# Batch 0 of the experts' layer computed for its chosen tokens only, its routing inside the first attention

## The chip, the cores and the metric

The kernel runs on one core of a Trainium2 chip. Its five engines (TensorE for matrix products, VectorE or DVE, ScalarE or ACT, GpSimd or POOL, and SyncE, which issues most DMAs) run their own instruction queues in order and meet at semaphores. The metric is the device time of one execution in microseconds (us), as the median of several.

## The reference

Two layers over `x` of shape (4, 512, 128). Each normalizes `x`, computes an attention `s` and a feed-forward gate `g` from it, and adds `s * silu(g)`. The change concerns the feed-forward part of the second layer, a mixture of 8 experts of which each token uses its best two:

```
xt = x.reshape(-1, d)                       # d = 128, 512 tokens for each of 4 batches
g = gelu(xt @ wg1 + bg1)
probs = softmax(g @ wg2)                    # 8 experts
top_vals, top_idx = top_k(probs, 2)
gates = zeros_like(probs).at[n, top_idx].set(top_vals)
h = gelu(einsum('nd,edh->enh', xt, w_in))   # hidden width 256
o = einsum('enh,ehd->end', h, w_out)
y = einsum('ne,end->nd', gates, o)
```

The first layer's attention works through segments of 64 tokens with a running memory (16 heads of 64); its own experts come before it. The second layer's attention has 16 heads of 8 and sums a softmax over 16 channels.

## The kernel before

The stages follow each other: the first layer's experts, the first attention, the second layer's experts, the second attention. A batch has 512 tokens in four tiles of 128. Nearly every instruction is issued through a helper (`mm1`, `act1`, `vec1`, `pool1`, `dma1`, lines 335 to 347) that keeps it in program order on its engine, so the order written in the code is the order of each queue.

**The first attention**, `attn0` (line 568), runs 32 segments, eight for each batch, in one loop. Segment n computes the scores of n+1, reads and updates the memory, attends, and turns the result of segment n-2. Segments with n % 4 other than 2 also hold four chunks of the projections of a later pair of tiles (values, keys, then queries); from segment 27 on there are none left. Segments with n % 4 = 2, from 6 on, end with an `output`, which adds two finished tiles to `x`. Work of the next stage is hung in with a table `between`: a key n means at the end of segment n, n - 0.5 ahead of its `attend`, n - 0.25 behind its chunks. PSUM is shared out by tags: "t" has two buffers of 512 values, "w" has three of 1024.

**The second layer's experts**, `begin_ffn1` (line 877), route a batch in steps: `sums`, `roots` and `scale` (statistics; `roots` is a square root on ACT), `normed`, `turned` (transposed on TensorE), `split` (three bf16 parts, on POOL), `hidden` (with GELU), `logits` (with an exponential), `chosen` (the best two, on DVE). From there two ways lead on.

- Batch 0 is dense: `up` and `down` (lines 1000 and 1010) compute all tokens for each of the eight experts, and DVE adds each expert's result with its weight (lines 1023 and 1025).
- Batches 1 to 3 compute chosen tokens: `placed` (line 1029) counts each token's place with its expert, `marked` (1051) makes 0/1 matrices from the places, `send` (1060) gathers the tokens of a tile with three bf16 products into 64 places per expert, `up2` and `down2` (1075 and 1086) compute two experts at once and write rows to DRAM, `fetch` (1103) reads each token's two rows back with indirect DMAs on POOL, and `joined` (1118) weighs and adds them on DVE. If an expert had more tokens in a tile than places, a flag starts another path at the end.

`ffn1` (line 1131) runs these as steps. A step issues its `up`, then what `between` holds for it, then the `down` of the step before, then what `between` holds half a step later. Before the change there are 20 steps: six dense ones, four of batch 1, two dense ones, four of batch 2, four of batch 3. The first `up` already stands in segment 31 of the attention. In between lie the routes of batches 2 and 3, the marks and sends of batches 1 to 3, the last `output` of the first attention, and fourteen calls of `prepare`, which make the second attention's operands of batch 0 and begin those of batch 1 (`prepare1`, line 1340: token products evicted on DVE, projections evicted on ACT, products of pairs on POOL, products of three (`cubes`) on DVE, and `forms` and `turned` on TensorE). All these use the PSUM tag "t" in turn with `down`, `logits` and `hidden`.

**The second attention**, `attn1`, runs 64 steps of one tile by four heads. Its table `rest` holds the fetches of batches 2 and 3 from steps 20 and 28 and their joins from 33 and 50. `gate1` applies the silu of a batch in the thirteenth step of that batch.

Of the kernel before, what the change touches and what calls it, by code (L numbers as in the profile page):

```python
# [21 lines left out]
P = 128  # L22
# [86 lines left out]
class Kernel:  # L109
# [767 lines left out]
    def begin_ffn1(self, pool, psum, layer, rooms=False):  # L877
# [31 lines left out]
        def chooses(b):  # L909
            return rooms and b > 0  # L910
# [140 lines left out]
        def marked(b, k):  # L1051

            t = marks[b, k] = self.f1b.tile(
                [P, NE, ROOM], BF16, name=name("one", b, k), tag="one", bufs=5
            )
            self.vec1(v.tensor_tensor(
                t, bc(places, 1, NE), bc(place[b][:, k], 2, ROOM), ALU.is_equal
            ))

        def send(b, k):  # L1060

            if k == 0:
                sent[b] = self.second1[b % 2].rearrange("p k (e s) -> p (k e) s", e=2).rearrange(
                    "p e (k s) -> p e k s", k=4
                )
                rows[b] = self.rooms.tile([NE * 4 * ROOM, D], F32, name=name("rows", b))
            ps = psum.tile([P, NE, ROOM], F32, name=name("px", b, k), tag="w", bufs=3)
# [5 lines left out]
            self.act1(sent[b][:, :, k], ps, AF.Copy)  # L1073

        def up2(b, i):
            ps = psum.tile([P, 2, 2, 4 * ROOM], F32, name=name("ph", b, i), tag="w", bufs=3)
            for e in range(2):
                for c in range(2):
                    self.mm1(
                        ps[:, e, c], lhsT=self.w_in[:, 2 * i + e, c * P : (c + 1) * P],  # L1080
                        rhs=sent[b][:, 2 * i + e], start=True, stop=True,
# [21 lines left out]
        def fetch(b, at, n=1):  # L1103

            if at == 0:
                acc[b] = self.of_batch("g", layer, b)
                got[b] = acc[b], (
                    self.first1[0][:, 0].rearrange("p (k d) -> p k d", k=4) if b == 1
                    else self.of_batch("xnT", layer + 4, b - 2)
                )  # L1110
# [20 lines left out]
    def ffn1(self, first, between, begun=False):  # L1131
# [4 lines left out]
        if begun:  # L1136
            dense = [(0, e) for e in range(NE)]
            own = [[(b, e) for e in range(NE // 2)] for b in range(B)]
            steps = dense[:6] + own[1] + dense[6:] + own[2] + own[3]
        for at, (b, e) in enumerate(steps):  # L1140
            up, down = (first.up2, first.down2) if begun and b else (first.up, first.down)
# [748 lines left out]
    def attn1(self, xnT, g1, rest):  # L1890
# [4 lines left out]
        with tc.tile_pool(name="a1", bufs=2) as self.a1, tc.tile_pool(  # L1895
# [70 lines left out]
            for i in range(n):  # L1966
# [3 lines left out]
                if t == 12:  # L1970
                    self.gate1(pool, g1[b], b)
# [333 lines left out]
    def run(self):  # L2305
# [15 lines left out]
        with tc.tile_pool(name="wf1", bufs=1) as wf1, tc.tile_pool(name="f1", bufs=1) as f1:  # L2321
# [7 lines left out]
            with tc.tile_pool(name="ap", bufs=1, space=PSUM) as psum:  # L2329
# [7 lines left out]
                    18: [(first.sums, 0)], 19: [(first.sums, 1)],  # L2337
                    20: [(first.roots, 0, 2)], 20.5: [(first.scale, 0, 2, False), (first.normed, 0)],
                    21: [(first.turned, 0), (first.normed, 1)],
# [134 lines left out]
```

## Time and profile before

| what | us |
|---|---|
| median of 3 runs | 721.2 (721.18 to 721.28) |
| the profiled execution | 722.03 |
| its span from first to last instruction | 720.4 |
| TensorE busy, of the span | 678.1 |
| one matmul of `down` or `down2` (320 in all) | 0.278 |
| one matmul of `up` / of `up2` | 0.595 / 0.379 |
| one indirect fetch on POOL | 0.95 to 1.39 |

A matmul's record overlaps with its neighbours', so the length of a group is read from the start of one group to the start of the next. In the groups of instructions a row gives the line, the engine, the operation, the tile written and the tile read, their shapes and the count; the time in brackets is what the engine waited before it, and for whom. Line 336 and line 339 are helpers, so instructions there are told apart by their tiles: `ph` is the product of `up`, `eo` that of `down`, `px` that of `send`, `lp` the logits, `pn` the places, `sc`, `mm`, `mu` and `dot` belong to a segment of the first attention, and `po` to its `output`. The experts' stage lies between 323 and 433 us of the span, the first attention between 84 and 326, the second from 433 on.

### The profile page before, as it was taken

How to read it: one execution, taken by the hardware profiler on the slowest of the kernel's cores; microseconds unless marked ns; L12 is line 12 of the kernel's file. 1: busy time of each engine (PE TensorE's matmuls, PEld its weight loads, DVE VectorE, ACT ScalarE, POOL GpSimd, SP SyncE). 2: the span in 40 equal slices, each digit the busy share in tenths (PEclk: the TensorE clock that was granted, in tenths of full speed). 3: DMA queues.
4: the chain of work that ended last, by engine and by line, in shares of the span. 5: the costliest groups of instructions: out<-in, count | busy, mean ns of one | idle time of the engine just before them, and what ended most of it. 6: DMA issues, size and time to landing. Idle time of an engine off the chain costs nothing.

```text
span 720.4 us, 23270 instructions
## 1 busy us (share of the span) xinstructions
PE 678.1 (94%) x9888; PEld 418.1 (58%) x9891; DVE 503.7 (70%) x1078; ACT 490.9 (68%) x809; POOL 345.7 (48%) x381
## 2 busy tenths in 40 slices
PE   7999879999999899979999999999999999999994
PEld 4666557878879677867777783332335233422433
DVE  6776365667576775884549324889896999588854
ACT  3423457877777885653563468989987899899830
POOL 7680027566666574693754423411482844312250
PEclk9999999999999998999999999999999999999999
DMA  7740143231331312100034249967949494955200
GB/s 184 135 134 0 56 129 79 67 106 40 97 106 33 105 30 78 39 12 1 1 98 153 74 146 213 255 168 174 240 148 221 109 250 129 217 143 144 59 17 19
DMA packets 84847, 79.42 MB, mean 110 GB/s; under 512 B 42512, under 2 KB 73520, under 8 KB 81664
## 3 DMA queue, kind: packets, MB, share of 16 engines
q1 hardware_dynamic: 81904, 75.12, 39.6%
q0 software_dynamic: 2256, 2.47, 1.8%
q8 instruction: 80, 1.31, 0.8%
q10 hardware_dynamic: 576, 0.26, 0.1%
q14 instruction: 31, 0.25, 0.1%
HBM read 51.62 MB, written 26.21 MB: 108 GB/s over the span
## 4 chain that ended last, share of the span: by engine, by line
PE 70%; DVE 12%; ACT 10%; issue 4%; DMA 2%; POOL 1%; SPq 0%; DVEq 0%; ACTq 0%; POOLq 0%
PE acc L336 9%; PE pp L336 8%; ACT e L339 7%; PE eo L336 7%; PE po L336 5%; PE ph L336 4%; PE b L336 3%; PE pv L336 3%; PE s L336 3%; PE pl L336 3%; PE sc L336 2%; PE pa L785 2%; PE pg L336 2%; PE pu L336 2%; PE dot L336 2%
## 5 line engine op out<-in xcount | busy, mean ns | idle before, releaser
L339 ACT ACTIVATE e<-s 128x1024 f32<-128x1024 f32 x124 | 121.9, 1056 | 13.8 <-PE s L336 12.7
L336 PE MATMUL acc<-e,strip 128*32 128x512 f32 x1000 | 124.6, 598 | 0.9 <-DVE e L1874 0.9
L339 ACT ACTIVATE e<-e 128x1024 f32<-128x1024 f32 x104 | 107.4, 1094 | 0.0
L736 POOL TENSOR_TENSOR t<-t,gate 128x512 f32<-128x512 f32 x32 | 49.7, 1554 | 66.0 <-DVE t L717 66.0
L336 PEld LDWEIGHTS acc<-e,strip 128*32 128x32 f32 x1000 | 28.6, 109 | 70.4 <-issue 59.2
L774 POOL TENSOR_TENSOR t<-t,gate 128x512 f32<-128x512 f32 x32 | 50.7, 1585 | 31.0 <-DVE sums L773 24.6
L339 ACT ACTIVATE pj<-pp 128x512 f32<-128x512 f32 x64 | 38.5, 602 | 21.2 <-PE pp L336 21.0
L684 DVE SCALAR_TENSOR_TENSOR elu<-elu,up 128x512 f32<-128x512 f32 x60 | 48.0, 801 | 5.3 <-ACT up L339 5.3
L661 DVE TENSOR_TENSOR E<-sc,cap 128x512 f32<-128x512 f32 x32 | 22.0, 688 | 40.2 <-PE sc L336 40.2
L339 ACT ACTIVATE h<-ph 128x1024 f32<-128x1024 f32 x20 | 20.5, 1023 | 38.3 <-PE ph L336 31.0
L339 ACT ACTIVATE attT<-pa 128x128 f32<-128x128 f32 x128 | 25.0, 284 | 28.5 <-PE pa L785 28.1
L336 PE MATMUL s<-q,k 64*128 64x512 bf16 x256 | 40.9, 382 | 3.5 <-ACT e L339 3.3
L336 PEld LDWEIGHTS <-k 64*128 64x128 bf16 x256 | 8.8, 94 | 59.6 <-issue 58.6
L775 POOL TENSOR_TENSOR t<-t,t 128x512 f32<-128x512 f32 x32 | 41.8, 1307 | 2.5
L336 PE MATMUL eo<-w_out,h 128*128 128x128 f32 x320 | 39.6, 278 | 0.0
L336 PEld LDWEIGHTS eo<-w_out,h 128*128 128x128 f32 x320 | 37.6, 192 | 3.4 <-issue 1.9
L339 ACT ACTIVATE elu<-pj 128x512 f32<-128x512 f32 x60 | 38.5, 642 | 0.1
L1714 POOL TENSOR_TENSOR pr<-pr,pr 128x512 f32<-128x512 f32 x14 | 22.5, 1629 | 33.4 <-DVE pr L1709 33.3
L339 ACT ACTIVATE up<-pj 128x512 f32<-128x512 f32 x60 | 38.4, 639 | 0.0
L336 PE MATMUL pp<-xnT,l0Wq 128*64 128x128 f32 x512 | 31.2, 277 | 3.2 <-ACT attT L339 2.2
L1623 DVE TENSOR_TENSOR second<-second,first 128x1024 f32<-128x1024 f32 x16 | 27.0, 1694 | 9.0 <-DMA second<-qf 9.0
L1157 POOL TENSOR_SCALAR th<-th 128x512 f32<-128x512 f32 x4 | 2.5, 617 | 64.2 <-ACT th L339 64.2
(331 smaller groups left out, 1641.9 us busy)
## 6 DMA issues: line engine op xcount, KB each, us to landing
vd<-vt SPq DMA_DIRECT2D x32, 256.0 KB
vone<-vd SPq DMA_DIRECT2D x64, 128.0 KB
first<-qe SPq DMA_DIRECT2D x8, 1024.0 KB
second<-qf SPq DMA_DIRECT2D x16, 512.0 KB
third<-qf SPq DMA_DIRECT2D x32, 256.0 KB
qf<-qT SPq DMA_DIRECT2D x64, 64.0 KB
k<-kd SPq DMA_DIRECT2D x16, 256.0 KB
q<-qd SPq DMA_DIRECT2D x16, 256.0 KB
```

The lines of the kernel that those rows point to most:

```text
L336: return self.pin(self.nc.tensor.matmul(*args, **kw))
L339: return self.pin(self.nc.scalar.activation(*args, **kw))
L661: self.vec1(nc.vector.tensor_tensor(e, ps[:, :, 0:256].rearrange("p x (hp c) -> p x hp c", hp=4), bc(bc(self.cap, 1, 4), 1, 2), ALU.min,))
L684: self.vec1(nc.vector.scalar_tensor_tensor(t, t, 1.0, up, ALU.min, ALU.add))
L736: nc.gpsimd.tensor_mul(t, t, self.gate)
L774: nc.gpsimd.tensor_mul(t, t, gate2)
L775: nc.gpsimd.tensor_add(t, t, seg[n]["t1"])
L785: self.pin(nc.tensor.transpose(ps[:, hp, :], seg[n]["att"][:, hp].rearrange("i p v -> i (p v)"), self.ident,))
L1157: self.pool1(self.nc.gpsimd.tensor_scalar(t, t, 0.5, 0.5, ALU.mult, ALU.add))
L1623: self.vec1(self.nc.vector.tensor_mul(t, t, self.first1[mm][:, two]))
L1714: self.nc.gpsimd.tensor_add(self.prod1[b, m], self.prod1[b, m], t)
```

## The change

Batch 0 takes the second way as well. The code of the diff, cut to its core:

```diff
         def chooses(b):
-            return rooms and b > 0
+            return rooms
...
         def marked(b, k):
-            t = marks[b, k] = self.f1b.tile(
-                [P, NE, ROOM], BF16, name=name("one", b, k), tag="one", bufs=5
-            )
+            if b == 0:
+                if k % 2 == 0:
+                    marks[b, -1] = self.top.tile(
+                        [P, 2, NE, ROOM], BF16, name=name("one", b, k), tag=f"g{k // 2}"
+                    )
+                t = marks[b, k] = marks[b, -1][:, k % 2]
+            else:
+                t = marks[b, k] = self.f1b.tile(
+                    [P, NE, ROOM], BF16, name=name("one", b, k), tag="one", bufs=5
+                )
...
         def send(b, k):
             if k == 0:
-                sent[b] = self.second1[b % 2].rearrange("p k (e s) -> p (k e) s", e=2).rearrange(
-                    "p e (k s) -> p e k s", k=4
-                )
+                if b:
+                    sent[b] = [self.second1[b % 2].rearrange("p k s -> p (k s)")]
+                else:
+                    sent[b] = self.wqkv[0:2]
+                each = NE // len(sent[b])
+                sent[b] = [t.rearrange("p (e k s) -> p e k s", e=each, k=4) for t in sent[b]]
...
-            ps = psum.tile([P, NE, ROOM], F32, name=name("px", b, k), tag="w", bufs=3)
+            tag, bufs = ("w", 3) if b else ("t", 2)
+            ps = psum.tile([P, NE, ROOM], F32, name=name("px", b, k), tag=tag, bufs=bufs)
...
-            self.act1(sent[b][:, :, k], ps, AF.Copy)
+            each = NE // len(sent[b])
+            for n, t in enumerate(sent[b]):
+                self.act1(t[:, :, k], ps[:, n * each : (n + 1) * each], AF.Copy)
...
             if at == 0:
                 acc[b] = self.of_batch("g", layer, b)
-                got[b] = acc[b], (
-                    self.first1[0][:, 0].rearrange("p (k d) -> p k d", k=4) if b == 1
-                    else self.of_batch("xnT", layer + 4, b - 2)
-                )
+                got[b] = [acc[b]]
+            if at == 4:
+                got[b].append(self.of_batch("xnT", layer + 4 + b // 2, b % 2))
...
-            dense = [(0, e) for e in range(NE)]
-            own = [[(b, e) for e in range(NE // 2)] for b in range(B)]
-            steps = dense[:6] + own[1] + dense[6:] + own[2] + own[3]
+            steps = [(b, i) for b in range(B) for i in range(NE // 2)]
...
-                if t == 12:
-                    self.gate1(pool, g1[b], b)
+                if t == 4 and b or i == n - 4:
+                    self.gate1(pool, g1[b - (t == 4)], b - (t == 4))
...
-                    18: [(first.sums, 0)], 19: [(first.sums, 1)],
-                    20: [(first.roots, 0, 2)], 20.5: [(first.scale, 0, 2, False), (first.normed, 0)],
-                    21: [(first.turned, 0), (first.normed, 1)],
-                    21.5: [(first.turned, 1), (first.split, 1)],
-                    21.75: [(first.hidden, 0), (first.hidden, 1)],
-                    23: [(first.logits, 0), (first.logits, 1), (first.chosen, 1)],
-                    24: [(first.placed, 1)], 25: [(first.chosen, 0)],
-                    30.5: [(first.up, 0, 0)],
+                    11: [(first.sums, 0)], 13.75: [(first.roots, 0, 1)],
+                    14: [(first.scale, 0, 1, False), (first.normed, 0)],
+                    15: [(first.turned, 0)], 16: [(first.split, 0)], 17.75: [(first.hidden, 0)],
+                    18.5: [(first.logits, 0)], 19: [(first.sums, 1)], 19.5: [(first.chosen, 0)],
+                    20: [(first.roots, 1, 2)], 20.5: [(first.scale, 1, 2, False), (first.normed, 1)],
+                    21: [(first.turned, 1), (first.placed, 0)],
+                    21.5: [(first.split, 1)], 21.75: [(first.hidden, 1)],
+                    22: [(first.marked, 0, 0)], 22.5: [(first.marked, 0, 1)],
+                    23: [(first.logits, 1)], 23.5: [(first.chosen, 1)],
+                    24.5: [(first.marked, 0, 2)], 25: [(first.placed, 1)], 25.5: [(first.marked, 0, 3)],
+                    26: [(first.send, 0, 0)], 27: [(first.send, 0, 1), (first.sums, 2)],
+                    28: [(first.send, 0, 2)], 28.75: [(first.roots, 2, 3)], 29: [(first.send, 0, 3)],
+                    30.5: [(first.up2, 0, 0)],
...
+                    1: [(f.scale, 2, 3, False), (f.normed, 2)],
+                    2: [(left[0],), (f.turned, 2), (f.split, 2)],
+                    3: [(f.hidden, 2), (left[1],), (begin,)] + marks(1, 0, 1, 2, 3),
+                    3.5: sends(1, 0, 1, 2, 3),
+                    4: [(f.logits, 2), (f.sums, 3), (f.chosen, 2)],
+                    5: [(f.roots, 3, 4)], 5.5: [(f.placed, 2)],
+                    6: marks(2, 0, 1) + [(f.scale, 3, 4, False), (f.normed, 3)],
+                    7: [(f.turned, 3)] + marks(2, 2, 3) + sends(2, 0, 1), 7.5: sends(2, 2, 3) + [(f.split, 3)],
+                    8: [(f.hidden, 3)], 9: [(f.logits, 3), (f.chosen, 3)],
+                    10.5: [(f.placed, 3)] + marks(3, 0, 1), 11: marks(3, 2, 3) + sends(3, 0, 1),
+                    11.5: sends(3, 2, 3), 13: [(self.operands1, 0, m) for m in range(3)],
+                    14: [(f.up2, B - 1, NE // 2 - 1), (self.opening1, psum, "w", 3)],
+                    15.5: [(self.opened1, psum, "w", 3)],
...
-                for k in range(14):
-                    between.setdefault(5 + k, []).append((prepare,))
+                for at in (4, 4, 5, 6, 6, 7, 8, 9, 9, 10, 10, 11, 12, 13):
+                    between.setdefault(at, []).append((prepare,))
                 for k in range(4):
-                    between.setdefault(13 + k, []).append((f.fetch, 1, 2 * k, 2))
+                    between.setdefault(7 + k, []).append((f.fetch, 0, 2 * k, 2))
...
-        for b, at, then in ((2, 20, 33), (3, 28, 50)):
-            for k in range(8):
+        for b, at, then in ((0, None, 13), (1, 4, 16), (2, 20, 33), (3, 28, 50)):
+            for k in range(8 if at else 0):
```

So the experts' stage has 16 steps of two experts each. The route of batch 0 lies in segments 11 to 25 of the first attention and its gather in 26 to 29, into the space of the query and key weights, whose last use is the projection in segment 25; the marks use the space of two gates that the first attention has used up. `sums` and `roots` of batch 2 also move into segments 27 and 29. The fetches of batch 0 stand in steps 7 to 10 of the experts, and those of batch 1 move from there to steps 4 to 11 of the second attention. The joins of batch 0 stand in steps 13 to 15 of the second attention; those of batch 1 move from the experts' stage to its steps 16 to 18. The gates of batches 0 to 2 are applied eight steps later than before.

More of the change, by code (lines that the diff above doesn't have):

```diff
@@ L1072, in send @@
                 )
-            self.act1(sent[b][:, :, k], ps, AF.Copy)
+            each = NE // len(sent[b])
+            for n, t in enumerate(sent[b]):
+                self.act1(t[:, :, k], ps[:, n * each : (n + 1) * each], AF.Copy)
         def up2(b, i):
             ps = psum.tile([P, 2, 2, 4 * ROOM], F32, name=name("ph", b, i), tag="w", bufs=3)
+            each = NE // len(sent[b])
             for e in range(2):
+                of = 2 * i + e
                 for c in range(2):
                     self.mm1(
-                        ps[:, e, c], lhsT=self.w_in[:, 2 * i + e, c * P : (c + 1) * P],
-                        rhs=sent[b][:, 2 * i + e], start=True, stop=True,
+                        ps[:, e, c], lhsT=self.w_in[:, of, c * P : (c + 1) * P],
+                        rhs=sent[b][of // each][:, of % each], start=True, stop=True,
                     )
@@ L1136, in ffn1 @@
         if begun:
-            dense = [(0, e) for e in range(NE)]
-            own = [[(b, e) for e in range(NE // 2)] for b in range(B)]
-            steps = dense[:6] + own[1] + dense[6:] + own[2] + own[3]
+            steps = [(b, i) for b in range(B) for i in range(NE // 2)]
         for at, (b, e) in enumerate(steps):
-            up, down = (first.up2, first.down2) if begun and b else (first.up, first.down)
+            up, down = (first.up2, first.down2) if begun else (first.up, first.down)
             if not begun or 0 < at < len(steps) - 1:
@@ L2379, in run @@
                 between = {
-                    1: [(f.sums, 2)], 2: [(left[0],)], 3: [(left[1],), (begin,)] + marks(1, 0, 1),
-                    4: marks(1, 2, 3) + [(f.sums, 3), (f.scale, 2, 4)] + sends(1, 0, 1),
-                    5: sends(1, 2, 3) + [(f.normed, 2), (f.normed, 3)],
-                    6: [(f.turned, 2), (f.split, 2), (f.turned, 3)],
-                    7: [(f.hidden, 2), (f.hidden, 3)],
-                    8: [(f.logits, 2), (f.logits, 3), (f.chosen, 2)],
-                    9.5: [(f.placed, 2), (f.split, 3)] + marks(2, 0, 1),
@@ L2387, in run @@
-                    10: marks(2, 2, 3) + [(f.chosen, 3)], 10.5: sends(2, 0, 1), 11: sends(2, 2, 3),
-                    12: [(f.placed, 3)], 13: marks(3, 0, 1), 14: marks(3, 2, 3) + sends(3, 0, 1),
-                    15: sends(3, 2, 3),
-                    17: [(self.operands1, 0, m) for m in range(3)],
-                    17.5: [(f.joined, 1, part) for part in range(3)],
-                    18: [(f.up2, B - 1, NE // 2 - 1), (self.opening1, psum, "w", 3)],
-                    19.5: [(self.opened1, psum, "w", 3)],
-                }
```

## Prediction

> **What bounds the kernel now.** I read the page's busy shares and its chain first, then busy time by stretch, then each engine's timeline where the change cuts in.
>
> ```profile
> PE 678.1 (94%) x9888; PEld 418.1 (58%) x9891; DVE 503.7 (70%) x1078; ACT 490.9 (68%) x809; POOL 345.7 (48%) x381
> ...
> PE 70%; DVE 12%; ACT 10%; issue 4%; DMA 2%; POOL 1%; SPq 0%; DVEq 0%; ACTq 0%; POOLq 0%
> ```
>
> TensorE is busy for 94% of the span and carries 70% of the chain that ended last, so removed TensorE work is worth its length wherever nothing else takes its place. Stretches (start:end, length, busy time per engine with counts, clock, DMA):
>
> ```profile
> 85.00:230.00 145.00, 139.15 (x3526) 111.83 (x3527) 93.32 (x200) 107.63 (x246) 85.54 (x59) 1.00 0.32 88
> 230.00:323.30 93.30, 84.17 (x2146) 69.41 (x2143) 71.69 (x197) 63.16 (x145) 60.62 (x45) 0.96 0.19 51
> 323.30:424.30 101.00, 97.66 (x877) 76.17 (x878) 53.10 (x175) 45.91 (x74) 45.01 (x43) 1.00 0.25 78
> ...
> 440.00:520.00 80.00, 77.12 (x938) 29.04 (x941) 65.08 (x82) 76.16 (x94) 22.90 (x22) 1.00 0.85 213
> ```
>
> These are the first attention (segments 0 to 19, then 19 to 31), the experts, and the start of the second attention. In the experts' stage TensorE works 97.7 of 101 us and DVE 53: there removed TensorE work counts. In the second row TensorE is idle 9 us at a clock of 0.96. In the last row TensorE and ACT are both over 95% and DVE at 81%.
>
> **What is removed (experts' stage).** TensorE's timeline (start, length, instructions):
>
> ```profile
> 327.92 1.95 PE L336 MATMUL eo<-w_out,h 128*128 128x128 f32 x16
> 329.71 1.88 PE L336 MATMUL ph<-xnT,w_in 128*128 128x512 f32 x4
> ...
> 351.61 1.89 PE L336 MATMUL ph<-second,w_in 128*128 128x256 f32 x8
> ```
>
> From start to next start a dense `up` takes 1.75 us and a `down` 1.81, so 3.56 per step. `up2` and `down2` take the same, for two experts. Batch 0 goes from eight steps to four: 4 x 3.56 = 14.2 us less. DVE also loses the 32 scalings of lines 1023 and 1025 (8.9 us), which lay beside TensorE.
>
> **What TensorE gets back.** `send` of batch 0: per tile three bf16 matmuls, 0.65 us (343.00 to 344.30 holds two tiles), 2.6 in all; `placed`: 0.1. Transposes, hidden layer and logits of batch 0 only move forward.
>
> **First attention.**
> - Square root and GELU now bring table loads for each batch alone: +6 loads here. At 13.75 and 17.75 they lie before an `output` (3.8 us of TensorE); in the same place of segment 18 ACT idles 3.12 us (229.8 to 232.96). The row: load 1.28, root 0.30, load 1.28, next activation at once, 2.87: hidden. Against it, the Trainium skill (ScalarE: Activation LUTs, "What ACT_TABLE_LOAD costs") prices each switch at 2.66 us with its drain, which would make 5.6 and cost 2.5 at each of the two places, +5. The trace shows no drain in 246.67 to 249.56; I take the row, 0. The roots at 20 stay, with their 2.21 us stall at 251.43.
> - `turned` of batch 0 in segment 15 needs a narrow PSUM buffer behind the value chunks, whose evictions wait for a DMA; the logits of segment 23 stalled 0.76 us there. +0.65. The position matrix `pn` behind the last key chunk: +0.25.
> - The logits of both batches stood together in segment 23 (timeline; in brackets the wait and for whom):
>
> ```profile
> 272.47 1.05 PE L336 MATMUL lp<-wg,gT 32*128 32x8 f32 x8 [0.76 <-ACT vt L339]
> 274.13 1.84 PE L336 MATMUL lp<-wg,gT 32*128 32x8 f32 x8 [0.60 <-DVE pb L970]
> ```
>
>   and the stretch just behind them (busy time per engine, then the clock, 0.50, and DMA):
>
> ```profile
> 274.00:277.00 3.00, 2.87 (x48) 2.88 (x52) 0.63 (x4) 0.77 (x3) 0.00 (x0) 0.50 0.25 90
> ```
>
>   The clock falls to 0.50 from 273.6 to 280.5: scores to `mu` take 0.4 us more each, 2.9 in all. Batch 0's logits go to 18.5 (0.96 us of TensorE), so the 0.60 wait and, I take it, the half clock go. `chosen` and marks of batch 0 lie in DVE's slack of 2 us per segment: +0.4; without that cover, 2.8 + 3.6. The logits of segment 23 thus start 0.65 + 0.25 + 0.96 + 0.4 = 2.3 later. What is late behind them is DVE: segments 24 to 26 cost it 3 x 5.05 us plus `chosen` 2.8, two marks 1.8, `placed` 2.5 and 1 of waits, 23.3. With 1.1 to the first read and 0.4 to the scores of segment 28 that is 24.8, against 28.8 now (272.47 to 301.26): -4.0, net -1.7 there.
> - `sums` of batch 2 comes from 326.97, where it was free, into segment 27. From 302 to 321 DVE runs without a break at 5.35 us a segment: +1.55, exposed. The sends in 26 to 29 fall beside DVE, in TensorE's idle 1.36 us per segment. The roots at 28.75 fit ACT's gap of 2.13 us at 314.8 but for 0.7, which DVE's delay covers.
> Sum: -1.7 + 1.55, and 0.5 for evictions in ACT's queue that I can't place: **+0.3**, between -1 and +4 (the half clock again).
>
> **Experts' stage: new waits.** I walked the new list step by step with the rows' durations. The narrow PSUM tag has two buffers, so each tile waits for the eviction of the last but one.
> - Step 2: `eo` behind the turned segment and the new transposes waits for ACT: 0.8.
> - Sends now stand after `down2`, directly ahead of the next `up2`, which waits for the eviction (0.6 plus two handovers): 0.9 or 1.0 at 3.5, 7.5 and 11.5, 2.8 in all. Before, a `down` covered it.
> - Step 4, the largest. `logits`, `sums`, `chosen`, two `prepare`, then `down2`. How long DVE takes for a choice (timeline, TensorE's logits of two batches first, then the first and last instruction of `chosen` on DVE):
>
> ```profile
> 366.17 1.95 PE L336 MATMUL lp<-wg,gT 32*128 32x8 f32 x16
> ...
> 368.94 0.18 DVE L977 TENSOR_REDUCE sm<-pb 128x4 f32<-128x32 f32 x1 [0.36 <-ACT pb L339]
> ...
> 371.67 0.17 DVE L994 COPY gates<-top 128x8 f32<-128x8 f32 x1
> ```
>
>   Logits to the end of `chosen`: 5.6 us; `sums` of batch 3 (1.6) in between adds 0.6. The key tokens of the first `prepare` are evicted on DVE behind that (0.6), and `down2` wants their buffer. TensorE has 2.8 us to do until then (`lp` 0.96, two token products 0.93 each): it stands 3.9 us. Queued behind: everything of steps 4 and 5.
> - Does the clock fall there? The rule (TensorE: Matmul & The Clock Gate, "What's actually happening") is half rate after an idle window of about 3.4 us, until a busy window has passed. The trace agrees that 2.21 us idle at 251.43 left the clock at 1.00, yet shows what the rule does not: 1.4 us of waits around thin matmuls at 272 brought 6.9 us of half clock, 2.9 lost. By the rule 3.9 us gives at most one window, -1.7; by the row 2.9. I take 2, range 0 to 3.
> - Step 5: `pn` behind `kT`, behind two table loads: 0.8 (0.39 stood at 374.86).
> - Steps 6 to 11: DVE carries `placed` (1.6), four marks (0.6 each alone, 1.05 beside POOL), `normed` (1.1), cubes (2.5 each) in two steps where it had three or four: the transpose 0.6, `forms` 0.6 and 0.6, `eo` behind the evictions of `turned` 1.45, the gather of batch 3 behind `cubes`, `placed`, `marked` 1.15.
> - Gone: 2.0 of the waits now at 355.17, 374.86 and 389.85.
> Sum: 0.8 + 2.8 + 3.9 + 2 + 0.8 + 4.4 - 2.0 = 12.7 back of 14.2, **-1.5**; the walk's own end (first scores at 421.4 instead of 424.33, the tokens of batch 1 done ahead of it, 1.0) gives -3.9. The parts round upwards; I take **-3.4**, from -7 (no clock, DVE never beside POOL) to +3 (all of it beside POOL).
>
> **Second attention.** DVE gets three joins more (before: at 419.6, free) in steps 13 to 18, six in all x 0.61. From 486.4 to 508.4 DVE has no gap. Two mixing buffers are freed 0.9 us later (TensorE's `mix` at 493.57 follows DVE within 0.1), `forms` at 511.7 0.8 later; DVE has 3.4 us of gaps from 513 to 520. Eight indirect fetches (POOL, 1.39 us each) move to steps 4 to 11; POOL has 23 us free there, but their rows share the DMA engines (0.85 busy): 0 to 1. I take **+1.3**, 0 to 4. The gates move within ACT's queue: 0. SP's queue: the table and part writes stand ahead of the row writes as before.
>
> **Sum.** +0.3 - 3.4 + 1.3 = -1.8 us, on the profiled execution's 722.0 (span 720.4 and 1.6 around it): 720.2. That execution lies 0.8 over the median of 721.2, so **719.4**.
>
> **Rivals.**
> - *The covers hold* (chance 0.25): the clock stays, step 4 waits 3 us, joins vanish in DVE's later gaps: 719.4 - 2 - 0.9 - 1.3 = 715.2. For it: DVE is at 53% in the stage. Against: the queue is in order, and step 4 follows from that.
> - *Hidden anyway* (0.12): the stage's end is set by batch 3's route (output, norm, logits, choice, marks), which the change doesn't shorten; TensorE only waits more: 721.2.
> - *DVE beside POOL becomes the bound* (0.33), ending slower: at 375 to 382 `placed` took 3.5 instead of 1.6 and marks 1.05 instead of 0.6; cubes at 455 took 5.1 instead of 2.5. POOL's quads, parts, splits and fetches now fall into the same steps 4 to 11. Two `placed` +1.9, eight marks +0.45 and one of the cubes +2.6 are 10 us on DVE; beyond the slack counted, 6 reach TensorE: 725.4. It decides from marks above 0.9 us and cubes above 3.5 in these steps.
> - The worked sum itself: 0.30, from 717.5 to 721.5.
>
> **How the numbers follow.** A measurement can tell about 0.2% (1.4 us) from no change: faster means under 719.8, slower over 722.6. Faster: the covers and two thirds of the worked sum, 0.45. Same: the rest of it and "hidden", 0.20 (a little taken from neighbours). Slower: 0.35. Range 713.5 to 727 takes in both outer cases; the worked sum's own range is 717.5 to 721.5.
>
> **What would show it.** `eo` after the two token products with a wait of about 4 us on DVE's `tokk`; a clock below 1 behind it and none at the logits of segment 23; waits near 0.9 at the first `up2` of batches 1 to 3; `sums` between segments 27 and 28; `mix` about 1 us late near the first batch's end. The forecast is wrong if the experts' stage shrinks by over 7 us or grows, or if the first attention moves by over 3.

## The result

| | before | after |
|---|---|---|
| median | 721.2 us (721.18 to 722.51, 6 runs) | 734.3 us (729.51 to 735.98, 6 runs) |
| profiled execution, and its span | 722.0, 720.4 | 735.5, 733.8 |
| start of the experts' stage (first `ph`) | 323.27 | 322.37 |
| experts' stage, to the first scores | 101.1 | 109.0 |
| second attention, first scores to the end of the span | 296.1 | 302.4 |

The change made the kernel slower: ratio 1.0168 (95% interval 1.0137 to 1.020). The forecast of 719.4 was 14.9 us too low, and the time lies outside its range of 713.5 to 727.

The page of the kernel after, busy time per engine and the chain that ended last:

```profile
PE 677.1 (92%) x9840; PEld 414.7 (57%) x9840; DVE 502.4 (68%) x1063; ACT 503.1 (69%) x827; POOL 369.1 (50%) x393
...
PE 25%; ACT 13%; DVE 3%; issue 2%; POOL 1%; DMA 0%; ACTq 0%; DVEq 0%; POOLq 0%
```

The chain could be followed back through less of the span than before, so its shares say little here. TensorE is busy as long as before, on less work. The same stretches as before the change (start:end, length, busy time per engine with counts, clock, DMA share, GB/s), the second and the third set to the stages of this trace:

```profile
85.00:230.00 145.00, 138.40 (x3503) 110.95 (x3504) 94.90 (x212) 110.12 (x248) 88.85 (x63) 1.00 0.31 88
230.00:322.40 92.40, 84.76 (x2181) 68.61 (x2178) 76.58 (x206) 70.88 (x159) 61.75 (x45) 1.00 0.19 53
322.40:431.40 109.00, 93.09 (x826) 74.35 (x826) 47.53 (x134) 47.19 (x76) 51.09 (x46) 0.95 0.26 82
440.00:520.00 80.00, 72.94 (x770) 25.89 (x762) 53.27 (x75) 64.97 (x79) 25.79 (x21) 0.96 0.75 187
```

The first attention went as forecast, and its clock is 1.00 throughout (0.96 before). In the experts' stage TensorE now idles 16 of 109 us and the clock is 0.95; in the fourth row TensorE, VectorE and ScalarE do less per us and the clock is 0.96 (shifted with the stage, to 447 to 527, the row has the same 72.94 us of TensorE). Part of the first loss had been forecast, the stall of step 4; most of the rest has one look. TensorE in the second attention (start, length, instructions, in brackets the wait and what ended it; `pl` is the product of `forms`, the preparation's 64 small matmuls):

```profile
470.89 0.74 PE L336 MATMUL pl<-feat,strip 128*32 128x64 f32 x33
471.89 0.42 PE L336 MATMUL pl<-feat,strip 128*32 128x129 f32 x4 [0.26 <-issue]
472.60 0.43 PE L336 MATMUL pl<-feat,strip 128*32 128x129 f32 x4 [0.29 <-issue]
...
477.25 0.38 PE L336 MATMUL pl<-feat,strip 128*32 128x129 f32 x3 [0.98 <-issue]
```

GpSimd at the same time:

```profile
470.93 0.95 POOL L1128 DMA_INDIRECT g<-rows,ids  x1 [0.30 <-issue]
472.18 1.57 POOL L1128 DMA_INDIRECT g<-rows,ids  x1 [0.30 <-issue]
```

An undisturbed `pl` group takes 1.54 us; this one takes 9.94. It waits for nothing that the profile shows ("issue"), four matmuls at a time, while the indirect fetches of batch 1 stand beside it. From 477.7 to 484.5, in the group and behind it, TensorE is at half clock. The groups at 374.61 (3.95 us, 0.70 of them a wait for VectorE) and 391.70 (6.58 us) in the experts' stage stand beside batch 0's fetches and look the same. The first and the fourth row of the second of them:

```profile
391.70 1.63 PE L336 MATMUL pl<-feat,strip 128*32 128x64 f32 x48 [0.60 <-DVE pb L970]
...
395.77 0.44 PE L336 MATMUL pl<-feat,strip 128*32 128x129 f32 x2 [1.09 <-issue]
```

Here the half clock lasts from 395.8 to 402.6. The trace of before had a first sign of it that the prediction passed over, beside its own fetches at 396 to 406:

```profile
405.72 0.79 PE L336 MATMUL pl<-feat,strip 128*32 128x64 f32 x18
407.65 1.35 PE L336 MATMUL pl<-feat,strip 128*32 128x64 f32 x46 [1.14 <-issue]
```

The step-4 stall, which was forecast, is there too: `eo` waits 3.73 us for `tokk` on VectorE, and takes 3.55 us where 1.95 is usual.

```profile
355.04 3.55 PE L336 MATMUL eo<-w_out,h 128*128 128x128 f32 x16 [3.73 <-DVE tokk L1386]
```

So there were two things to test: the waits of the experts' steps, and the long `pl` groups.

### The profile page after: what moved, and what is told of

Its sections match the earlier page's. It is cut to its first block, busy times and chain, and to the rows that moved or that the text cites. A ratio compares the mean times of both kernels' runs of the same rounds, so it can differ in the third digit from the quotient of the medians.

```text
span 733.8 us, 23188 instructions
## 1 busy us (share of the span) xinstructions
PE 677.1 (92%) x9840; PEld 414.7 (57%) x9840; DVE 502.4 (68%) x1063; ACT 503.1 (69%) x827; POOL 369.1 (50%) x393
## 5 line engine op out<-in xcount | busy, mean ns | idle before, releaser
L336 PE MATMUL acc<-e,strip 128*32 128x512 f32 x1000 | 126.2, 605 | 0.9 <-DVE e L1887 0.9
L336 PE MATMUL pl<-feat,strip 128*32 128x129 f32 (+1 forms) x1024 | 33.0, 251 | 11.1 <-issue 9.4
L336 PE MATMUL eo<-w_out,h 128*128 128x128 f32 x256 | 35.3, 296 | 5.3 <-DVE tokk L1386 3.7
L336 PEld LDWEIGHTS eo<-w_out,h 128*128 128x128 f32 x256 | 33.1, 208 | 8.9 <-DVE tokk L1386 3.9
L339 ACT ACTIVATE attT<-pa 128x128 f32<-128x128 f32 x128 | 25.0, 285 | 14.6 <-PE pa L785 14.2
L336 PEld LDWEIGHTS pl<-feat,strip 128*32 128x32 f32 x1024 | 22.6, 110 | 21.8 <-issue 18.8
```

Source lines behind the costliest of these rows:

```text
L336: return self.pin(self.nc.tensor.matmul(*args, **kw))
L339: return self.pin(self.nc.scalar.activation(*args, **kw))
```

## The experiments

**Theory 1:** indirect fetches that stand beside `forms` break up its stream of instructions. **Rival 2:** the bytes on the DMA engines do it, looked up or not. **Rival 3:** VectorE beside GpSimd is late with the features. The runs came in five sets, each on one chip (A to E) with the kernel before beside it (medians 721.5, 717.2, 720.6, 719.9 and 720.0 us). The kernel after was run again on C alone; 734.3 and the stage lengths 109.0 and 302.4 are of the first measurement. Stage lengths are of the profiled execution, which can lie some us off the median (plain fetches on A: 726.8 for 722.6), the second attention here to the start of the last output matmul (before 288.9, after 296.7); "long" are the `pl` groups with issue gaps, of those that have two or more fetches beside them. Where all but one or two are long, the exception is the first group of the experts' stage, which takes 2.60 to 4.17 us through a wait for VectorE, half clock or both, and on E one more of 1.97 us.

| kernel | chip | ratio to before (95%) | experts | second attention | long groups |
|---|---|---|---|---|---|
| plain fetches | A | 1.0027 (1.0009 to 1.0045) | 103.0 | 290.9 | only batches 2, 3 |
| fetches later | A | 1.0162 (1.0125 to 1.0199) | 104.5 | 296.0 | second attention |
| step 4 | A | 1.0109 (1.0071 to 1.0147) | 103.2 | 297.5 | all but one |
| before, fetch moved | A | 1.0102 (1.0051 to 1.0153) | 99.3 | 293.0 | two |
| gated | B | 1.0115 (1.0087 to 1.0143) | 102.8 | 290.0 | none |
| gated, all batches | B | 1.0131 (1.0104 to 1.0158) | 102.8 | 293.8 | none |
| steps | B | 0.9941 (0.9919 to 0.9964) | 95.2 | 287.6 | none |
| steps and gated | B | 1.0017 (1.0003 to 1.0031) | 94.8 | 294.6 | none |
| after, again | C | 1.0210 (1.0192 to 1.0229) | 109.3 | 297.0 | all |
| steps | C | 1.0038 (1.0016 to 1.0060) | 97.7 | 296.2 | all but one |
| plain fetches | C | 1.0057 (1.0027 to 1.0086) | 103.0 | 288.4 | only batches 2, 3 |
| steps and plain | C | 0.9970 (0.9952 to 0.9989) | 97.6 | 289.5 | only batches 2, 3 |
| gates | D | 1.0233 (1.0214 to 1.0253) | 105.4 | 300.9 | one, slightly |
| steps and gates | D | 1.0086 (1.0061 to 1.0111) | 95.1 | 299.2 | one, slightly |
| steps | D | 1.0063 (1.0038 to 1.0089) | 97.7 | 296.5 | all but one |
| gates, second try | E | 1.0112 (1.0084 to 1.0139) | 105.3 | 292.5 | none |
| steps and gates, second try | E | 0.9977 (0.9963 to 0.9992) | 96.2 | 290.6 | none |
| steps | E | 1.0056 (1.0037 to 1.0075) | 97.9 | 295.0 | all but two |

### Plain fetches

```diff
             for m in range(at, at + n):
                 c, k = m // 4, m % 4
+                if b < 2:
+                    src = rows[b].rearrange("(m p) d -> m p d", p=P)
+                    self.pool1(nc.gpsimd.dma_start(out=got[b][c][:, k], in_=src[m]))
+                    continue
```

> Leaves out the gather of batches 0 and 1: each tile of rows is read in order by a plain DMA on the same queue (GpSimd) at the same place, not each token's own row, so the same bytes are moved and nothing is looked up. Theory 1 (the indirect fetches starve TensorE's stream of instructions while the 64 small matmuls and 64 weight loads of `forms` stand beside them): the issue gaps in the pl groups at about 391-398 us and 470-480 us go, the half clock behind them goes, the experts' stage falls from 109.0 to about 102-103 us and iteration 7 to 8 of the second attention from 14.4 to about 7 us; about 720-722 us in all. Rival 2 (it is the bytes on the DMA engines that count, looked up or not): both gaps stay, 733-736 us. Rival 3 (VectorE beside GpSimd holds the features back): the gaps stay, since GpSimd issues as before and VectorE's work is the same, 732-736 us.

As theory 1 has it, the gaps of batches 0 and 1 are gone, at 722.6 us. One trace shows both cases. TensorE where plain transfers of batch 0 run (1.54 us, undisturbed), and later where batch 2's fetches, still indirect, do:

```profile
393.88 1.54 PE L336 MATMUL pl<-feat,strip 128*32 128x64 f32 x64 [0.60 <-DVE pb L970]
...
536.17 1.55 PE L336 MATMUL pl<-feat,strip 128*32 128x64 f32 x51
538.06 0.41 PE L336 MATMUL pl<-feat,strip 128*32 128x129 f32 x4 [0.34 <-issue]
```

The queue of GpSimd's DMAs in the 4 us around the undisturbed group (392 to 396; packets, MB, share of the 16 engines):

```profile
q0 software_dynamic: 192, 0.39, 33.1%
```

In the same stretch of the kernel after, where the group at 391.70 is long, it is less:

```profile
q0 software_dynamic: 108, 0.21, 21.0%
```

More packets and bytes from the same queue leave the group alone when they come from plain transfers, so rival 2 falls; rival 3 falls with it, as VectorE's work is the same. GpSimd had issued these transfers by 393.85, just ahead of the group; plain ones issued inside a group follow below.

### Fetches later in the program

```diff
-                    between.setdefault(7 + k, []).append((f.fetch, 0, 2 * k, 2))
+                    between.setdefault(12 + k, []).append((f.fetch, 0, 2 * k, 2))
...
-        for b, at, then in ((0, None, 13), (1, 4, 16), (2, 20, 33), (3, 28, 50)):
+        for b, at, then in ((0, None, 13), (1, 10, 20), (2, 20, 33), (3, 28, 50)):
```

> Same work, only later places: batch 0's fetches at the experts' steps 12 to 15 in place of 7 to 10, batch 1's at iterations 10 to 17 of the second attention in place of 4 to 11, its sums at 20 to 22 in place of 16 to 18. Theory 1: no `forms` group stands beside a fetch any more, so both gaps go: experts' stage about 102-103 us, second attention about 297 us, 720-723 us in all. Rival 2 (bytes): the gaps move to whatever stands beside the fetches then and about the same is lost, 731-736 us. Rival 3 (VectorE beside GpSimd): the same as rival 2, since the number of fetches is the same, perhaps 3 us less.

Half of it happened, and the median stayed at 732.2 us. Six of batch 0's fetches ran at 430 to 437, and the experts' stage became 4.5 us shorter. Its group at 392.90 begins 0.6 us after GpSimd has issued the other two, while 33 of the queue's packets still move, and takes 1.54 us: fetches in flight alone did not stretch it. Batch 1's ran at 462.7 to 470, beside `forms` at 466.3 as before: GpSimd had nothing to wait for there, so a later place in the program changed nothing in time. The group took 7.4 us.

### Step 4

```diff
-                    4: [(f.logits, 2), (f.sums, 3), (f.chosen, 2)],
+                    4: [(prepare,), (prepare,), (f.logits, 2), (f.sums, 3), (f.chosen, 2)],
```

> Only step 4 of the experts is put in another order: its two pieces of preparation ahead of `logits`, `sums` and `chosen` of batch 2, not behind them, so that the top-k on VectorE no longer stands ahead of what the next piece's copy of tokens needs. The prediction's step (a stall of 3.7 us there, shown as a wait of eo on tokk, and about 1.7 us of half clock behind it): 729-731 us, with the wait at about 355 us under 1 us. If the stall was covered by something that ends at the same time: 733-736 us.

As expected: 729.7 us, the experts' stage 5.8 us shorter than in the first trace of the kernel after, `eo` at 352.34 without a wait. A wait of 1.61 us ahead of `pn` on the choice's mask took its place.

### The kernel before with batch 1's fetches moved beside `forms`

```diff
-                for k in range(4):
-                    between.setdefault(13 + k, []).append((f.fetch, 1, 2 * k, 2))
...
-        for b, at, then in ((2, 20, 33), (3, 28, 50)):
+        for b, at, then in ((1, 4, 16), (2, 20, 33), (3, 28, 50)):
```

> The kernel before, with nothing changed but the place of batch 1's eight fetches: from the experts' steps 13 to 16 to iterations 4 to 11 of the second attention (as in the kernel after), its sums at iterations 16 to 18. Theory 1: the `forms` group at iteration 7 to 8 now stands beside fetches and shows the issue gaps and the half clock: second attention from 296 to about 301-303 us, less some 1-2 us of fetches and sums taken from the experts' stage, so 724-727 us. Rival 2 and 3: bytes and VectorE's work are the same as before and only moved, 720-722 us.

The median is 726.7 us, as theory 1 has it, but the four runs lie between 721.4 and 731.9, and the profiled one is the fastest, with a single gap of 0.33 us in its group, which takes 2.69. So the trace doesn't show where the others lost their time, nor whether long groups differ from one execution to the next.

### Gates, first set, and the reordered steps

The gated kernels put batch 1's fetches behind the gate's tanh, for which GpSimd does wait, and batch 0's and its sums elsewhere; the lines for batch 1:

```diff
+        for b, at, then in ((0, None, 8), (1, 13, 20), (2, 20, 33), (3, 28, 50)):
...
-                if t == 4 and b or i == n - 4:
+                if t == 4 and b > 1 or i in (12, n - 4):
```

> The second attempt at moving the fetches of batches 0 and 1 away from `forms`, since the first one moved batch 1's only in the program's order: GpSimd had nothing to wait for and issued them at the same time as before. Now batch 0's are at the experts' steps 12 to 15, its sums at iterations 8 to 10, its gate at iteration 12 (as in the kernel before), and batch 1's fetches at iterations 13 to 16, so that they stand on GpSimd behind the gate, which waits for ScalarE's tanh; its sums at 20 to 22. Theory 1 (indirect fetches beside `forms` cost): no gap in the pl groups of batches 0 and 1, second attention about 290-291 us from the first scores to the last output (after: 295.8, before: 288.0), all in all 721-724 us. If batch 1's gaps come from something else that stands there (the table writes, the sums on VectorE): they stay, 728-732 us.

> As the run before it, and batches 2 and 3 also have their fetches moved off `forms`: to iterations 28 to 31 and 44 to 47, two each, sums of batch 2 at 36 to 38. The kernel before has batches 2 and 3 beside `forms` as well and loses little there (gaps of 0.5 us listed, in the kernel after 0.3 to 0.6 us four times). Theory 1: 1 to 3 us less than the run before it, 719-722 us, and no issue gap in any pl group. Rivals: the same as the run before it, within 1 us.

The steps kernel moves no fetch:

```diff
-                    3.5: sends(1, 0, 1, 2, 3),
-                    4: [(f.logits, 2), (f.sums, 3), (f.chosen, 2)],
-                    5: [(f.roots, 3, 4)], 5.5: [(f.placed, 2)],
-                    6: marks(2, 0, 1) + [(f.scale, 3, 4, False), (f.normed, 3)],
-                    7: [(f.turned, 3)] + marks(2, 2, 3) + sends(2, 0, 1), 7.5: sends(2, 2, 3) + [(f.split, 3)],
+                    3.5: sends(1, 0, 1, 2, 3) + [(prepare,)],
+                    4: [(prepare,), (f.logits, 2), (f.sums, 3), (f.chosen, 2)],
+                    5: [(f.roots, 3, 4)],
+                    6: [(f.placed, 2)] + marks(2, 0, 1) + [(f.scale, 3, 4, False), (f.normed, 3)],
+                    7: marks(2, 2, 3) + sends(2, 0, 1) + [(f.turned, 3)], 7.5: sends(2, 2, 3) + [(f.split, 3), (prepare,)],
...
-                    11.5: sends(3, 2, 3), 13: [(self.operands1, 0, m) for m in range(3)],
+                    11.5: sends(3, 2, 3) + [(prepare,)], 13: [(self.operands1, 0, m) for m in range(3)],
...
-                for at in (4, 4, 5, 6, 6, 7, 8, 9, 9, 10, 10, 11, 12, 13):
+                for at in (5, 6, 6, 7, 9, 9, 10, 10, 11, 13):
```

> No fetch moved; only the experts' steps in another order: a piece of preparation behind the last two sends of each batch (steps 3.5, 7.5, 11.5) so that TensorE has work while ScalarE evicts what the next up2 needs; step 4's other piece ahead of logits, sums and chosen; placed(2) behind step 6's up2; turned(3) behind the sends at step 7. Of the prediction's list: the stall of step 4 (3.7 and about 1.7 of clock) goes as in the run of step 4 alone (-4.5 us), the three waits of 0.69 to 0.78 us ahead of up2 go (-2.2), the wait on mask of 1.6 us that the run of step 4 alone had goes, and of the lnt waits behind normed(3) (2.0) about half. 725-728 us. If these waits lie beside something that is late anyway: 729-731 us.

> Both together: the experts' steps reordered as in the run before it and all fetches moved off `forms`. If the costs add up, 734.3 - 11.7 (fetches beside forms, batches 0 and 1) - 1.5 (batches 2 and 3) - 7.5 (waits at the experts' steps) = 713.6: 713-717 us, under the kernel before by 4 to 8 us, which is what the prediction's walk over TensorE's work gave the change without its stalls. If something else ends at the same time as what these relieve (the load of tables, VectorE), 718-722 us.

This set surprised. The gated kernels and both changes together missed their brackets (725.0, 727.0 and 719.1 us), though the kernel before ran 4 us faster on B than on A. The steps kernel, at 712.8 where 725 to 728 was expected, was faster than the kernel before, and its trace has no long group, though its fetches stand beside `forms`. TensorE first, then GpSimd:

```profile
384.77 1.54 PE L336 MATMUL pl<-feat,strip 128*32 128x64 f32 x64 [0.60 <-DVE pb L970]
```

```profile
383.61 0.95 POOL L1128 DMA_INDIRECT xnT<-rows,ids  x1 [0.30 <-issue]
384.87 0.95 POOL L1128 DMA_INDIRECT xnT<-rows,ids  x1 [0.30 <-issue]
386.12 0.95 POOL L1128 DMA_INDIRECT xnT<-rows,ids  x1 [0.30 <-issue]
```

No group in the four traces of chip B had an issue gap; the changed kernel itself was not run there. And the moves had a price: with all fetches gated, the second attention is 7 us longer than with the steps alone (294.6 for 287.6). One part of it is in view: the sums of batch 0, moved from iterations 13 to 15 to 8 to 10, stand on VectorE ahead of what TensorE's table products need. VectorE, then TensorE in the trace of steps and gated:

```profile
465.54 0.69 DVE L1135 TENSOR_TENSOR g<-g,gates 128x512 f32<-128x512 f32 x1
466.14 0.19 DVE L1565 TENSOR_SCALAR lin<-pf 128x36 f32<-128x36 f32 x1
```

```profile
466.87 0.66 PE L336 MATMUL b<-second,lin 64*32 64x512 f32 x7 [2.42 <-DVE lin L1565]
```

### The changed kernel, steps and plain fetches on one chip

> The changed kernel itself, once more and beside the next three on one chip. In the second set of runs no group of `forms` was interrupted at all, not even where indirect fetches stood beside it (five such groups in the run of the reordered steps, all 1.54 us), while in the first set, on another chip, every such group was. Theory 1 as it stands (indirect fetches beside `forms` always cost): ratio to the kernel before 1.015 to 1.018, groups of 4 to 10 us. Theory 1b (the same, but only on some chips, or in some placements of the program in memory): here either all overlapped groups are long and the ratio is 1.015 to 1.018, or all are 1.54 us and the ratio is 1.003 to 1.007.

> The reordered experts' steps with the fetches where the change has them, as run in the second set. If the ratio of 0.994 there was due to the order alone (the reordering also keeps the refills of the instruction queue out of `forms`), it is 0.994 here whatever the run of the changed kernel beside it shows. If it was due to the chip (theory 1b), it stands about 0.009 to 0.011 (6.5 to 8 us: the step 4 stall, the waits ahead of up2 and on the mask) under the changed kernel beside it: 1.006 if that is 1.017, 0.994 if that is 1.004.

> The fetches of batches 0 and 1 as plain transfers, as in the first set (rows in order, so the gather is left out). Where the changed kernel beside it shows long groups of `forms`: ratio 1.001 to 1.004 again, and no long group in batches 0 and 1. Where it shows none: the same as the changed kernel within 0.2%, since then there is nothing to gain but GpSimd's shorter issue (0.53 us for 1.26).

> Reordered steps and plain fetches of batches 0 and 1 (the gather left out there) together. If the two costs add up: 0.990 to 0.994 of the kernel before on a chip that shows the long groups, and the same as the reordered steps alone on one that doesn't.

It is as theory 1b has it: on chip C every overlapped group of the steps kernel but one is long, and its ratio is 1.0038, against 0.9941 on chip B. So the order of the steps alone does not keep the groups short; nor does it keep loads of instructions out of them, as one packet of an instruction queue falls into the group at 384.77 on B, which takes 1.54 us. Each chip was used in one set only, so whether it is the chip or something else of its set isn't shown. All four ratios missed their brackets, the changed kernel's by 0.3 points on the slow side, and the reordered steps gained 1.7 points on it for 0.9 to 1.1. On C plain fetches take 12.7 us off the changed kernel, the reordered steps also 12.7, and both together 18.4: they overlap, as the reordered steps alone also leave the group in the experts' stage shorter. Plain transfers issued inside a group leave it alone too, here in the trace of steps and plain, TensorE, then GpSimd:

```profile
459.18 1.54 PE L336 MATMUL pl<-feat,strip 128*32 128x64 f32 x64
```

```profile
458.71 2.11 POOL L1130 DMA_DIRECT2D xnT<-rows  x4
```

One group of the changed kernel here takes only 1.94 us and yet costs as much. TensorE, then what ACT waits for:

```profile
471.29 0.65 PE L336 MATMUL pl<-feat,strip 128*32 128x64 f32 x32
472.10 1.13 PE L336 MATMUL pl<-feat,strip 128*32 128x129 f32 x32 [0.16 <-issue]
```

```profile
479.99 0.52 ACT L339 ACTIVATE forms<-pl 128x192 f32<-128x192 f32 x1 [6.43 <-remote]
```

By its records the product had ended at 473.2, but ACT went on only at 479.99, and so did VectorE, 1.8 us after GpSimd had issued the last of batch 1's fetches. TensorE itself ran on, to 475.7. So by these records what comes late is not an operand but TensorE's signal that it is done; the profile doesn't name what ended the wait, and no run tests it further.

### Gates that wait for `forms`

```diff
+                def gated(b):
+                    t = self.late.tile([P, 1], F32, name=f"behind{b}")
+                    self.pool1(self.nc.gpsimd.tensor_copy(t, self.now1[b]["ones"][:, 3:4]))
...
-                for k in range(4):
-                    between.setdefault(7 + k, []).append((f.fetch, 0, 2 * k, 2))
+                between.setdefault(12, []).extend([(gated, 0), (f.fetch, 0, 0, 4), (f.fetch, 0, 4, 4)])
...
+        rest[11] = [(gated, 1)]
+        for b, k, at in (
+            (1, 0, 0), (1, 4, 1), (2, 0, 11), (3, 0, 12), (2, 4, 16), (3, 4, 29),
+        ):
+            rest.setdefault(at, []).append((first.fetch, b, k, 4))
```

> The changed kernel with only the places of its fetches changed, and now held back on GpSimd by something it has to wait for: a copy of one column that reads what the last `forms` of the batch left (128x1, one ahead of batch 0's fetches at step 12, one at iteration 11). Batch 0's eight then stand behind the experts' last `forms`, batch 1's at iterations 0 and 1, half of batches 2 and 3 behind the second attention's last `forms` of batch 1, the rest at 16 and 29; the sums stay where the change has them (13, 16, 33, 50), as the earlier attempt lost some us to moved sums. Theory 1b on a chip that shows long groups: every `forms` group 1.54 us (but those that wait for VectorE's features), 11 to 15 us under the changed kernel there, ratio to the kernel before 0.998 to 1.004. On a chip without long groups: 1.003 to 1.008, as the fetches cost nothing there.

> The same with the experts' steps reordered. On a chip with long groups: 0.982 to 0.990 of the kernel before (the run with plain fetches of batches 0 and 1 and reordered steps had 0.997 and still 6 us of long groups in batches 2 and 3); without them: 0.990 to 0.996, as the reordered steps alone had. If fetches cost the same wherever they stand (rival 2), about 1.004, as the reordered steps alone had beside the changed kernel's 1.021.

> The reordered steps with the fetches left beside `forms`, for comparison on the same chip: 1.002 to 1.006 and long groups, or 0.992 to 0.996 and none.

The times missed: 1.0233 and 1.0086. The issue gaps were gone but for 0.2 us; GpSimd, however, stood behind a tile that was still read:

```profile
453.50 1.18 POOL L1128 DMA_INDIRECT xnT<-rows,ids  x1 [15.54 <-PE ptq L336]
```

Behind it were queued the key casts of batch 1, and the tables came late. The second try:

```diff
-            (1, 0, 0), (1, 4, 1), (2, 0, 11), (3, 0, 12), (2, 4, 16), (3, 4, 29),
+            (1, 0, 0), (1, 4, 11), (2, 0, 12), (2, 4, 16), (3, 0, 29), (3, 4, 30),
```

> The gated places again, with the fault of the run before mended: batch 1's second four fetches write into the tile that holds its own normalised tokens, and GpSimd stood 15.5 us behind the projection that still reads it, with the key casts of batch 1 queued behind. They now stand behind the gate of iteration 11, batch 2's at 12 and 16, batch 3's at 29 and 30. On a chip where the reordered steps beside it show long groups: no `forms` group with an issue gap, no wait of GpSimd on ptq, second attention 287 to 291 us from the first scores to the last output, ratio 1.000 to 1.008. If the fetches cost as much where they stand now (rival 2): 1.016 to 1.022 like the changed kernel.

> The same with the reordered steps: 0.984 to 0.992 of the kernel before on a chip with long groups (reordered steps with long groups 1.004 to 1.006, less some 11 to 14 us of long groups and half clock), 0.990 to 0.996 on one without; 1.002 to 1.006 by rival 2.

> The reordered steps with the fetches beside `forms`, for comparison on the same chip: 1.002 to 1.006 with long groups, 0.992 to 0.996 without.

On chip E, which shows long groups in the steps kernel, moving the fetches takes 6.0 us off it (723.75 to 717.72) and leaves no issue gap. A part of the long group in the experts' stage of the steps kernel, then the same group with gates:

```profile
385.39 0.64 PE L336 MATMUL pl<-feat,strip 128*32 128x129 f32 x4 [1.13 <-issue]
```

```profile
388.17 1.54 PE L336 MATMUL pl<-feat,strip 128*32 128x64 f32 x64 [0.60 <-DVE pb L970]
```

Indirect fetches cost beside `forms`, not wherever they stand. Both ratios still miss their brackets, by 0.3 and 0.6 points. In the second attention 4.4 us of the gain arrived, in the experts' stage only 1.7: the long group at 383.28 (5.07 us) is 1.54 now, but behind a wait of 1.56 us for VectorE's features, which both kernels have, the clock fell to half from 371.1 to 378.0 in the gated one alone. (All eight traces with this order of steps have that wait of 1.56 us; three show half clock there.) With gates, the reordered steps are worth 10.0 us (727.73 to 717.72).

The last kernel, with the change in it, is 0.23% under the kernel before (0.08 to 0.37%) on a chip with long groups. On one without, the reordered steps alone are 0.59% under it.

## Why the prediction was wrong

- **First attention, +0.3.** It ended 0.9 earlier instead. The half clock at 273.6 to 280.5 is gone as forecast; over the traces this point varies from 320.9 to 325.3, so a us can't be read here.
- **Experts' stage, the listed waits.** In the trace of the changed kernel they come nearly item by item: `eo` of step 2 0.92 for 0.8; the three waits ahead of `up2` 2.17 for 2.8; step 4 3.73 for 3.9; `pn` 0.89 for 0.8; VectorE's lateness in steps 6 to 11 4.5 for 4.4, though otherwise shared out: the transposes lost 2.06 and not 0.6, because four normalisations beside GpSimd took 3.58 us. The clock cost of step 4 was 1.7 (half rate for 3.4 us) for 2. The rule that the prediction cites there from the Trainium skill (TensorE: Matmul & The Clock Gate, "What's actually happening": half rate after an idle window) fits this row.
- **The stage's sum, -3.4.** It was too low even without the fetches. Where no group of this stage was long it measured 103.0 (plain fetches, A and C) and 102.8 (gated, B), 1.7 to 1.9 longer than before; less the 0.9 of batch 1's tokens, which the prediction counted as gained, that is about 4 us of the miss. The gated trace, then that of the reordered steps on the same chip (start:end, length, busy time per engine with counts, clock, DMA share, GB/s):

```profile
323.91:426.67 102.76, 89.78 (x824) 71.68 (x823) 47.96 (x134) 47.30 (x76) 44.54 (x40) 0.97 0.26 83
```

```profile
323.64:418.88 95.24, 86.45 (x824) 70.31 (x823) 51.05 (x134) 47.06 (x76) 51.62 (x46) 1.00 0.30 92
```

  The waits in all are not at fault: in the first row TensorE is idle 13.0 us, before 3.3, so 9.6 more, where the prediction's list gives 10.7. But the half clock costs 3.3 us, for 2: there are two windows of 3.4 us, one behind step 4 and one behind the late transposes. And at full clock, in the second row, TensorE is busy 11.3 us less than before (97.7), where 14.2 less those tokens is 13.3: a group behind a wait takes 0.1 longer (`eo` 2.05 for 1.95), and four transposes that wait one by one take 1.3 where four together take 0.6. The remaining 1.9 lies in taking -3.4, near the walk's -3.9, when the list itself came to -1.5.
- **The failed step: the fetches.** This is the larger part of the miss. The prediction put them at "0 to 1" in the second attention, as a matter of rows that share the DMA engines, and gave those in the experts' steps 7 to 10 no line in its sum. Measured by leaving them out: plain fetches gave back 12.7 us of the median on C, and 11.7 on A against the first measurement. In the experts' stage that is 6.0 us (109.0 to 103.0) and 6.3 on C; in the second attention 5.8 (296.7 to 290.9) and 8.6 on C (297.0 to 288.4). In the rows of the changed kernel the stage has 5.0 us more in one group, 1.7 in another and 2.2 of half clock behind (`eo` 3.78 for 1.95, `ph` 2.29 for 1.89), more than the 6 that came back: without them the gather of batch 3 waits 1.43 for 0.47, and a second window of half clock appears (376.0 to 379.4 on A). In the second attention one group took 8.4 us more. About 12 for the fetches and 4 for the stage's sum, less 1.2 for the first attention, are the 15 that the forecast missed.
- **The joins and late mixing, +1.3.** Not settled: with plain fetches the second attention is 288.4 and 290.9, before 288.9, of which the tokens of batch 1 (0.9) have moved into the experts' stage.
- **Rivals.** "The covers hold" fell with the stall of step 4. "DVE beside POOL becomes the bound" had the right side, and its signs came mixed: one of the cubes took 4.4 us (378.60 to 383.02), above its 3.5, but the marks 0.85 and 0.64, below its 0.9; it put 6 us on VectorE, and counted the fetches only as work of GpSimd beside it. "Hidden anyway" fell as the reordered steps shortened the stage by 11.6 us.

What stays open: why an indirect fetch holds back TensorE's instructions and signals where a plain transfer of the same size on the same queue doesn't, and why on chips A, C, D and E but not on B (each in one set of runs). Only the place, the kind of transfer, the order of the steps and the chip were varied.

## What to carry to other kernels

Look for "issue" gaps inside dense groups of tiny matmuls, and for what GpSimd issues beside them: a gap of 1.14 us in the profile of before was the first sign of a loss of about 12. Moving an operation later in the program moves little or nothing in time on an engine that has nothing to wait for, as with batch 1's fetches; it has to be gated, and each tile that it writes must be free by then, or the queue behind it pays. In front of a step that waits for another engine's eviction, place a piece of independent work: with step 4's order that was worth 5.8 to 12.7 us here, in five pairs of runs. A wait costs more than its length where it cuts a dense group or brings half clock.

## What the runs showed of the hardware

- A `pl` group (64 matmuls and 64 weight loads, 1.54 us) beside two or more indirect fetches of 128 rows had issue gaps and took 1.9 to 9.9 us in most cases on four chips, and had none on a fifth (1.54 us undisturbed); beside plain transfers it took 1.54 us, also with four issued inside it.
- In one trace ACT and VectorE went on 6.8 us after the recorded end of the product that they waited for.
- An indirect fetch holds GpSimd for 1.26 us from start to start, a plain one for 0.53.
- Gaps of 0.3 to 1.0 us each, 3.2 us in 6.8, came ahead of half clock; no single one was longer than 0.98 us. A wait of 1.56 us was followed by half clock in three of eight traces with the same order of steps. The half clock lasted 3.4 or 6.8 us each time in these stages.
